# A two-layer graph attention network on one core: two more aggregates split on two levels, and the second-level left sums made in halves from a pool of their own

## The chip, the cores and the metric

The kernel runs on one core of one Trainium2 chip. The metric is the device time of one execution in microseconds. One execution was also taken by the hardware profiler; its page and its trace are what this document reads. The engines are TensorE (PE; its weight loads are PEld), VectorE (DVE), ScalarE (ACT), GpSimd (POOL) and SyncE (SP). Each engine takes its own list of instructions in order. In this kernel SP issues the loads, and POOL issues nearly all the stores and some of the loads.

## The reference

```python
h = jnp.maximum(_layernorm(x), 0.0)            # x: 2708 x 1024, float32
f = h @ Wf + bf;  g = h @ Wg + bg
scores = where(adj > 0, relu(f @ g.T), NEG)
x = x + softmax(scores, axis=1) @ (h @ W + bW)
h = jnp.maximum(_layernorm(x), 0.0)
h2 = h @ W1
scores = where(adj > 0, leaky_relu(h2 @ a1 + (h2 @ a2).T, 0.2), NEG)
out = x + relu(softmax(scores, axis=1) @ h2)
```

Everything is float32; adj is a 2708 x 2708 matrix of zeros and ones.

## The kernel before, in words

**Panels and products.** The kernel works with transposed attention matrices: the 2708 destination rows are the columns of five panels p = 0 to 4, with 576, 576, 532, 512 and 512 columns, and the source rows stand on the partitions, as ten pairs of 128-row tiles (q = 0 to 9) and a small rest (`left_over`). The large matrix products use a scheme with seven half-size products, M1 to M7, in place of eight, whose operands are sums and differences of the quarters. Two matmul records in the trace stand for one float32 matmul.

**Layer 0.** For each panel: `scores(p)` (products sx, sy, sz, ten steps q), then `project_q(p+1)` for the next panel's right side, then `aggregate(0, p)` (attention times h, products gx, gy, gz, gv), then `project(0, p)` (times W, plus residual and bias, result x1). project(0,3) stands after scores(4). In `scores`, VectorE's work is held in program order (`nc.hold`).

**Aggregates.** `aggregate` uses one level of seven products: each has ten pairs q by four blocks d, with a right side of half the panel's width h. Its left rows come by SP from DRAM (`hc`), where `rows_h` and `sums_h` put the seven sums of each pair (`hg_d`, one array for two pairs). `aggregate_quartered` splits each of the seven products into seven again: five blocks k by two blocks d, with a right side of h/2. `quarters_of` makes its right sides, and its left sides are rows (`hr_d`) or sums of four quarters of rows (`hs2_d`). Before the change it serves panels 1 to 4 of layer 1 only.

**Second-level left sums.** `put_quarters(m, k)` is one such task: POOL loads four quarter rows (`hq<-hr_d`), VectorE makes four additions of 128x256 (`add` and `sub`), POOL stores the result (`hs2_d`, in the profile `hs_d<-hq`). There are 7 x 5 = 35 tasks, with two loads and two stores of 256 KB each. They lie in the list `lazy`, from which `behind` takes work behind a stage's matmuls while `spare[0]` is set. The rows of layer 1 are written by `pair_h` (sums g1, g2: `g` in the profile, and `hr_d<-g`) as soon as `finish0` has a pair of finished x1 rows. One block k needs the rows of two neighbouring pairs.

**Order.** A list scheduler reorders what isn't held in program order, within what buffers and data allow. Buffers of a pool go round in the order of the program. The pools are `slots` (54 buffers, work tiles), `strm` (12, what is streamed in: hc, As, w, hq and others) and a few small ones.

**Residual.** `finish0` loads x (SP), and POOL adds the bias to it in SBUF by an accumulating DMA; the projected rows are then added and stored to x1.

Of the kernel before, what the change touches and what calls it, by code (L numbers as in the profile page):

```python
# [57 lines left out]
def kernel(  # L58
# [60 lines left out]
    strm = ctx.enter_context(tc.tile_pool(name="strm", bufs=12))  # L119
# [8 lines left out]
    def stream(name, shape=(P, D), dt=FP):  # L128
        return strm.tile(list(shape), dt, tag="strm", name=name)

# [23 lines left out]
    groups = [[q, q + 1] for q in range(0, NQ, 2)]  # L154
    group_of = {q: (i, j) for i, g in enumerate(groups) for j, q in enumerate(g)}
    assert sorted(group_of) == list(range(NQ))
    hg_d = [dram.tile([P, 7, len(g), W], FP, name=f"hg_d{i}") for i, g in enumerate(groups)]
    NK = NQ // 2
    WH = W // 2
    hr_d = dram.tile([P, 7, 2, 2, NK, WH], FP, name="hr_d")  # L160
    hs2_d = dram.tile([P, 7, 4, NK, WH], FP, name="hs2_d")

    def rows_at(m, q):

        return hr_d[:, m, :, q % 2, q // 2]
# [30 lines left out]
    spare, from_slots = [False], [False]  # L196
# [4 lines left out]
    def one(of=None):  # L201
        of = later if of is None else of
        for it in of[:4 if of is lazy and from_slots[0] else ahead[0]]:
            if it[1]:
                it[1]()
                it[1] = None
        us, _, go = of.pop(0)[:3]
        go()
        return us
# [114 lines left out]
    def pair_h(q, ha, hb):  # L324

        n = P
        on = nc.vector
        if q >= NQ - F // 2:
            s1, s2, s3, s4 = (slot(f"g{i}")[:, :W] for i in range(4))
            for m, h in ((M1, ha[0]), (M2, hb[0]), (M4, hb[1])):  # L330
                store(rows_at(m, q), as_blocks(h))
            on.tensor_tensor(s1, ha[1], hb[1], OP.add)
            on.tensor_tensor(s2, s1, ha[0], OP.subtract)
            for m, h in ((M5, s1), (M6, s2)):
                store(rows_at(m, q), as_blocks(h))

            def rest():
                on.tensor_tensor(s4, hb[0], s2, OP.subtract)
                on.tensor_tensor(s3, ha[0], ha[1], OP.subtract)
                for m, h in ((M3, s4), (M7, s3)):  # L340
                    store(rows_at(m, q), as_blocks(h))
            return rest
        g1, g2 = stream("g1", (P, 2, W)), stream("g2", (P, 2, W))
        s1, s2, s3, s4 = g1[:n, 0], g1[:n, 1], g2[:n, 0], g2[:n, 1]
        on.tensor_tensor(s1, ha[1], hb[1], OP.add)
        on.tensor_tensor(s2, s1, ha[0], OP.subtract)
        on.tensor_tensor(s3, ha[0], ha[1], OP.subtract)
        on.tensor_tensor(s4, hb[0], s2, OP.subtract)
        for m, h in ((M1, ha[0]), (M2, hb[0]), (M4, hb[1])):
            store(rows_at(m, q), as_blocks(h))  # L350
        store(rows_at(slice(M5, M6 + 1), q), as_blocks(g1[:n]))
        store(rows_at(slice(M7, M3 + 1), q), as_blocks(g2[:n]))

    def rows_h(q, ha, hb):

        i, j = group_of[q]
        for m, h in ((M1, ha[0]), (M5, ha[1]), (M2, hb[0]), (M4, hb[1])):
            store(hg_d[i][:, m, j], h)
# [3 lines left out]
    def sums_h():  # L362

        def fetch(q, two):
            i, j = group_of[q]
            for m in (M1, M2):
                two.append(stream("hr", (P, 2, W)))
                load(two[-1], hg_d[i][:, m:m + 2, j])

        def first(q, two):  # L370
            (a0, a1), (b0, b1) = ((t[:, 0], t[:, 1]) for t in two)
            add(b1, a1, b1)
            sub(a1, a0, a1)

        def second(q, two):
            (a0, a1), (b0, b1) = ((t[:, 0], t[:, 1]) for t in two)
            sub(a0, b1, a0)
            sub(b0, b0, a0)
            i, j = group_of[q]
            store(hg_d[i][:, M6:M7 + 1, j], two[0])  # L380
            store(hg_d[i][:, M3, j], b0)
            store(hg_d[i][:, M5, j], b1)
            summed[0] += 1
        for q in range(NQ):
            two = []
            put(1.4, lambda q=q, two=two: first(q, two), lambda q=q, two=two: fetch(q, two))
            put(1.4, lambda q=q, two=two: second(q, two))

    BY_QUARTERS = (M1, M5, M2, M6, M7, M3, M4)
    made_quarters = {}  # L390

    def put_quarters(m, k, to=lazy):

        two = []

        def fetch():
            if from_slots[0]:
                two.extend(slot(f"hq{h}", (P, 2, WH)) for h in range(2))
            else:
                t = stream("hq", (P, 4, WH))  # L400
                two.extend(t[:, 2 * h:2 * h + 2] for h in range(2))
            for h in range(2):
                nc.gpsimd.dma_start(two[h], hr_d[:, m, h, :, k])

        def go():
            a11, a12, a21, a22 = (two[h][:, i] for h in range(2) for i in range(2))
            add(a22, a21, a22)
            sub(a21, a11, a21)
            sub(a11, a22, a11)
            sub(a12, a12, a11)  # L410
            for h in range(2):
                store(hs2_d[:, m, 2 * h:2 * h + 2, k], two[h])
            made_quarters[m] = made_quarters.get(m, 0) + 1
        put(1.7, go, fetch, to=to)

    def quarters_until(m):
        while made_quarters.get(m, 0) < NK:
            one(lazy if lazy else later)
# [465 lines left out]

    def aggregate(l, p, S, sm, then={}, rate=3.0):
# [28 lines left out]
        def left(m, q, d):  # L914
            i, j = group_of[q]
            if (m, i) not in hc:
                hc[m, i] = stream("hc", (P, 4, WH) if l else (P, 2, W))
                load(hc[m, i], hr_d[:, m, :, :, i].rearrange("p h f c -> p (h f) c") if l else hg_d[i][:, m])
            return hc[m, i][:, d // 2 * 2 + j, d % 2 * P:(d % 2 + 1) * P] if l else hc[m, i][:, j, d * P:(d + 1) * P]
# [67 lines left out]
    def quarters_of(p, S):  # L987
# [9 lines left out]
        def operand(m, q):  # L997
            if m in (M5, M4):
                return t1(q)
            s = wa_(q) if m in (M1, M6, M7) else wb_(q)  # L1000
            return s[:, hi if m in (M3, M7) else lo]
# [27 lines left out]
        def second():  # L1029
            for q in range(NQ):  # L1030
                sub(wa_(q)[:, lo], wb_(q)[:, hi], t1(q))
            for q in range(NQ):
                sub(wa_(q)[:, hi], wb_(q)[:, hi], wa_(q)[:, hi])

        def fourth():
            for q in range(NQ):
                sub(t1(q), wb_(q)[:, lo], wa_(q)[:, lo])
        return {"make": make, "right": right, "first": first, "fifth": fifth, "second": second, "fourth": fourth}

    def aggregate_quartered(p, S, sm, of_right, then={}, fine=1.2):  # L1040
# [12 lines left out]
        def product(m, n, ps, start):  # L1053
            quarters_until(m)
            if (m, 0) not in lasts:
                for i, of in enumerate((hr_d[:, m, :, :, NK - 1].rearrange("p h f c -> p (h f) c"), hs2_d[:, m, :, NK - 1])):
# [5 lines left out]
            load(t, hr_d[:, m, i // 2, i % 2, :NK - 1] if raw else hs2_d[:, m, i, :NK - 1])  # L1062
# [11 lines left out]
        def left_over(banks, e, s, fresh):  # L1074

            two = stream("hl", (P, W + 2 * P))
            load(two, hgl_d[1][:, e])
# [44 lines left out]
        def with_second():  # L1122
# [3 lines left out]
        before_next = {M1: lambda: make(M5), M5: with_second, M2: lambda: (of_right["fourth"](), make(M6)), M6: lambda: make(M7),  # L1126
                       M7: lambda: make(M3), M3: lambda: make(M4)}
        left_out = None
        for m in BY_QUARTERS:
            V = [quad(*direct[m])[:, 2 * r:2 * r + 2] for r in range(2)] if m in direct else [v[:, :, :h] for v in in_pairs("V")]  # L1130
# [40 lines left out]
            if m == M5:  # L1171
                of_right["second"]()
            if m == M5:
                inverse.append(inverse_sums(p, sm))
# [178 lines left out]
    def scores(p, B):  # L1353
# [49 lines left out]
        for q in range(NQ):  # L1403
# [3 lines left out]
            if q + 2 <= LEFT:  # L1407
                fetch(q + 2)
            sa, sb = slot("Sa"), slot("Sb")
# [111 lines left out]
    def rows_done(t, xt):  # L1521
# [14 lines left out]
        if panel_of[t] == NP - 1:  # L1536
# [9 lines left out]
            else:  # L1546
# [12 lines left out]
                if q == NQ - 1:  # L1559
                    for m in BY_QUARTERS:  # L1560
                        put_quarters(m, q // 2, later)
# [17 lines left out]
        elif whole:  # L1579
# [3 lines left out]
            if quads_met[q // 2] == 2:  # L1583
                put(0.0, lambda: [put_quarters(m, q // 2) for m in BY_QUARTERS])
# [8 lines left out]

    def finish0(p):
        xs, seen = {}, {}

        def start(ts):
            for t in ts:
                if p == NP - 1:
                    first_mask[t] = load_mask(0, *pair_of[t])  # L1600
                if t == TINY:
# [7 lines left out]
                xs[t] = row_halves("x_res", t == MONO)  # L1609
                load_rows_of(t, xs[t], x)  # L1610
# [27 lines left out]

    got = {}
# [29 lines left out]
    for p in range(NP):  # L1669
        got["S"], got["acc"] = scores(p, B)  # L1670
# [20 lines left out]
        spare[0], from_slots[0] = p > 0, p == NP - 1  # L1691
        G[p] = aggregate(0, p, S, got["sm"], then)
        spare[0] = False
        if p == 0:
            flush()
            ahead[0] = 2
# [98 lines left out]
    for p in range(NP):  # L1795
# [6 lines left out]
        g = aggregate_quartered(p, S, sm, next_right, then, fine=1.0) if p else aggregate(1, p, S, sm, then, rate=4.0)  # L1802
# [34 lines left out]
```

## Time and profile before

| | |
|---|---|
| median of 3 runs | 3094.57 us (3094.34 to 3098.68) |
| the profiled execution | 3099.78 us, its span 3098.0 us |
| TensorE busy | 3002.8 us, 97% of the span |
| VectorE, ScalarE, POOL busy | 2070.7, 463.2, 506.3 us |
| DMA | 764.70 MB, mean 247 GB/s; SP's queue 62.0% and POOL's 16.4% of 16 engines' span |
| mean granted TensorE clock | 0.989 |

The span runs from the first to the last instruction; the execution's own time has 1.8 us around it. Busy times are shares of one execution, and the stages differ: the stretches of the span have to be read one by one, cut where the stages change. The layer-0 aggregates of panels 2 and 3 lie at 1262 to 1399 us and 1639 to 1771 us. Releasers in the profile are inferred from semaphore events, and a pair of names such as `hq<-hr_d` is output and input of an instruction.

### The profile page before, as it was taken

Reading aid. Unit: us, or ns where it says so; the run is one execution under the profiler, and the core shown is the slowest. Engines: PE = TensorE matmul, PEld = TensorE weight load, DVE = VectorE, ACT = ScalarE, POOL = GpSimd, SP = SyncE. Lnnn points to the kernel's source line nnn. Section 1 sums busy time; section 2 is a strip of 40 time slices with the busy share of each in tenths; the row PEclk is TensorE's granted clock in tenths of the full one; section 3 lists DMA queues with packets and bytes.
Section 4 is the critical chain, followed back from the end, with each engine's and each line's share of the span. In section 5 each row is a group of like instructions: output and inputs, shape, how many; then the busy total and the mean of one; then the engine's idle time right before and its main releaser. Section 6 shows DMA issues by size and latency. Waiting matters only on the chain.

```text
span 3098.0 us, 41680 instructions
## 1 busy us (share of the span) xinstructions
PE 3002.8 (97%) x14630; PEld 2298.1 (74%) x14630; DVE 2070.7 (67%) x4615; ACT 463.2 (15%) x817; POOL 506.3 (16%) x786
## 2 busy tenths in 40 slices
PE   8998999899999999999999999997999999999998
PEld 4576777657877588885888886783777969879694
DVE  5767693776651596716975277766968768887853
ACT  3420020010110101101011001301222121212200
POOL 1421101310011110214101001141202010020202
PEclk9999999999999999999999999998999999999999
DMA  6999967998565796758967577789667868888896
GB/s 225 291 257 254 301 247 253 309 274 229 178 238 153 217 260 223 244 158 241 278 199 255 164 217 234 237 266 350 229 216 249 274 202 296 287 269 294 264 297 246
DMA packets 448577, 764.70 MB, mean 247 GB/s; under 512 B 175776, under 2 KB 262592, under 8 KB 448368
## 3 DMA queue, kind: packets, MB, share of 16 engines
q1 hardware_dynamic: 393008, 598.31, 62.0%
q0 software_dynamic: 55360, 163.73, 16.4%
q8 instruction: 116, 1.90, 0.3%
q14 instruction: 93, 0.76, 0.1%
HBM read 627.95 MB, written 133.91 MB: 246 GB/s over the span
## 4 chain that ended last, share of the span: by engine, by line
PE 71%; DVE 11%; DMA 7%; issue 7%; SPq 2%; POOL 1%; ACT 1%; POOLq 0%; DVEq 0%; ACTq 0%
PE sz L1378 6%; PE gx L661 6%; PE gy L661 6%; PE gz L661 5%; PE gz L1067 5%; PE pz L1267 4%; PE sx L1378 4%; PE sy L1378 4%; PE px L1267 4%; PE py L1267 3%; PE gx L1067 3%; PE gy L1067 3%; PE M_ps L574 3%; PE qz L661 2%; PE qx L661 2%
## 5 line engine op out<-in xcount | busy, mean ns | idle before, releaser
L1378 PE MATMUL sz<-B,As 128*128 128x288 f32 (+2 forms) x1200 | 293.5, 394 | 11.8 <-DVE st L45 8.8
L1378 PEld LDWEIGHTS sz<-B,As 128*128 128x128 f32 x1200 | 227.8, 191 | 61.8 <-DVE st L45 12.7
L1378 PE MATMUL sx<-B,As 128*128 128x288 f32 (+2 forms) x800 | 199.6, 392 | 6.4 <-DMA As<-hs_d 4.4
L1378 PE MATMUL sy<-B,As 128*128 128x288 f32 (+2 forms) x800 | 199.3, 392 | 2.3 <-DMA As<-hs_d 2.3
L661 PE MATMUL gz<-Sa,hc 128*128 128x288 f32 (+2 forms) x800 | 189.2, 397 | 6.3 <-DMA hc<-hg_d 6.3
L661 PEld LDWEIGHTS gz<-Sa,hc 128*128 128x128 f32 x800 | 153.8, 193 | 40.1 <-DMA hc<-hg_d 6.8
L1378 PEld LDWEIGHTS sx<-B,As 128*128 128x128 f32 x800 | 151.3, 190 | 40.1 <-DMA As<-hs_d 3.7
L1378 PEld LDWEIGHTS sy<-B,As 128*128 128x128 f32 x800 | 152.0, 190 | 33.4 <-issue 2.7
L1067 PE MATMUL gz<-quarter,hc 128*128 128x128 f32 (+2 forms) x1344 | 168.8, 279 | 3.8 <-DVE gT L45 3.7
L143 POOL DMA_DIRECT2D out_dram<-x_res x180 | 89.0, 501 | 482.1 <-DVE x_res L45 474.7
L1067 PEld LDWEIGHTS gz<-quarter,hc 128*128 128x128 f32 x1344 | 160.6, 191 | 5.1 <-DVE gT L45 4.6
L1267 PE MATMUL px<-w,gT 128*128 128x512 f32 x320 | 143.9, 602 | 7.5 <-DMA w<-in_L_gnn_W_dram 6.0
L1267 PE MATMUL pz<-w,ps 128*128 128x512 f32 x320 | 142.1, 594 | 0.8 <-DVE pt L45 0.8
L1267 PE MATMUL py<-w,ps 128*128 128x512 f32 x320 | 142.0, 593 | 0.0
L143 POOL DMA_DIRECT2D mk_d<-mask x55 | 35.8, 652 | 534.8 <-DVE mask L45 528.1
L1267 PEld LDWEIGHTS px<-w,gT 128*128 128x128 f32 x320 | 60.9, 193 | 80.9 <-issue 74.7
L1267 PEld LDWEIGHTS pz<-w,ps 128*128 128x128 f32 x320 | 60.2, 190 | 77.1 <-issue 70.7
L1267 PEld LDWEIGHTS py<-w,ps 128*128 128x128 f32 x320 | 60.5, 190 | 75.8 <-issue 73.9
L574 PE MATMUL M_ps<-wgT,wfT 128*128 128x512 f32 x256 | 113.5, 600 | 1.6 <-ACT hsT L45 1.6
L661 PE MATMUL gy<-T,hc 128*128 128x288 f32 (+2 forms) x480 | 111.6, 394 | 0.0
L977 POOL TENSOR_TENSOR gT<-gT,rr 128x2304 f32<-128x2304 f32 (+5 forms) x12 | 44.4, 3700 | 382.4 <-DVE rr L45 179.8
L661 PEld LDWEIGHTS gy<-T,hc 128*128 128x128 f32 x480 | 91.2, 190 | 19.5
(377 smaller groups left out, 5803.6 us busy)
## 6 DMA issues: line engine op xcount, KB each, us to landing
hc<-hg_d SPq DMA_DIRECT2D x175, 512.0 KB
As<-hs_d SPq DMA_DIRECT2D x150, 512.0 KB
hc<-hr_d SPq DMA_DIRECT2D x119, 512.0 KB
hc<-hs_d SPq DMA_DIRECT2D x112, 512.0 KB
w<-wt_d SPq DMA_DIRECT2D x96, 512.0 KB
w<-in_L_gnn_W_dram SPq DMA_DIRECT2D x72, 512.0 KB
md<-md_d SPq DMA_DIRECT2D x56, 512.0 KB
adj_i<-in_adj_dram SPq DMA_DIRECT2D x200, 128.0 KB
```

The lines of the kernel that those rows point to most:

```text
L143: nc.gpsimd.dma_start(a, b)
L574: nc.tensor.matmul(ps, wfT[a][c // NH][:, c % NH, :], wgT[b][c], start=(c == 0), stop=(c == NC - 1))
L661: nc.tensor.matmul(ps[d], left(m, k, d), right(m, k), start=(start and k == 0), stop=(k == K - 1), skip_group_check=True)
L977: nc.gpsimd.tensor_tensor(of(e, s), of(e, s), by(s, k), OP.mult)
L1067: nc.tensor.matmul(ps[:, d], lhs[:, d * P:(d + 1) * P], inner_right(m, n, k), start=(start and k == 0 and d == 0), stop=(k == NK - 1), ski ...
L1267: nc.tensor.matmul(ps, left[i][m][:, k, :], w_[k], start=(start and k == 0), stop=(k == NH - 1), skip_group_check=True)
L1378: nc.tensor.matmul(ps[:n, :h], lefts[q][:, i % 2, c, :n], B[m][c // 2][:, c % 2, :h], start=(start and c == 0), stop=(c == NH - 1), skip_g ...
```

## The change

- The layer-0 aggregates of panels 2 and 3 are made by `aggregate_quartered`. M1 and M5 stay one-level products (through `accumulate`), and M2, M6, M7, M3 and M4 are split again. `quarters_of` loses the separate buffer for M4's right side.
- The rows of layer 0 move from `hg_d` to `hr_d[0]`, in the layout of layer 1 (pieces of 1 KB in place of 2 KB), and layer 0 gets second-level sums of its own, `hs2_d[0]`. Their tasks are queued after aggregate(0,0) in the program's text; `spare[0]` is set again after aggregate(0,1).
- `put_quarters` makes each task in two halves of 128 columns: one load and one store by POOL of 256 KB, four additions of 128x128, in a buffer from a new pool `side` with four buffers. Layer 1 has 70 such half-tasks, layer 0 has 50. At most three are fetched ahead.
- `strm` has 10 buffers in place of 12. `from_slots` goes.
- For panels 2 and 4 (`ORDERED`) the residual is prepared in DRAM during `scores`: POOL copies x to x1_d and adds the bias there by accumulating DMAs, in program order, and `finish0` loads the sum by SP.

The diff, cut to its core (the moves from `hg_d` to `hr_d[0]` in `rows_h`, `sums_h` and `aggregate` only change the address):

```diff
-    strm = ctx.enter_context(tc.tile_pool(name="strm", bufs=12))
+    strm = ctx.enter_context(tc.tile_pool(name="strm", bufs=10))
+    side = ctx.enter_context(tc.tile_pool(name="side", bufs=4))
...
-    hr_d = dram.tile([P, 7, 2, 2, NK, WH], FP, name="hr_d")
-    hs2_d = dram.tile([P, 7, 4, NK, WH], FP, name="hs2_d")
+    hr_d = [dram.tile([P, 7, 2, 2, NK, WH], FP, name=f"hr{l}_d") for l in range(2)]
+    hs2_d = [dram.tile([P, 7, 4, NK, WH], FP, name=f"hs2{l}_d") for l in range(2)]
...
-        for it in of[:4 if of is lazy and from_slots[0] else ahead[0]]:
+        for it in of[:3 if of is lazy else ahead[0]]:
...
-    BY_QUARTERS = (M1, M5, M2, M6, M7, M3, M4)
+    BY_QUARTERS = [(M2, M6, M7, M3, M4), (M1, M5, M2, M6, M7, M3, M4)]
...
+    def put_quarters(l, m, k, to=lazy):
+        for half in range(2):
+            two = []
+            cs = slice(half * P, (half + 1) * P)
+
+            def fetch(two=two, cs=cs):
+                two.append(aside("hq", (P, 4, P)))
+                nc.gpsimd.dma_start(two[0].rearrange("p (h f) c -> p h f c", h=2), hr_d[l][:, m, :, :, k, cs])
+
+            def go(two=two, cs=cs):
+                a11, a12, a21, a22 = (two[0][:, i] for i in range(4))
+                add(a22, a21, a22)
+                sub(a21, a11, a21)
+                sub(a11, a22, a11)
+                sub(a12, a12, a11)
+                store(hs2_d[l][:, m, :, k, cs], two[0])
+                made_quarters[l, m] = made_quarters.get((l, m), 0) + 1
+            put(0.9, go, fetch, to=to)
...
         def second():
             for q in range(NQ):
-                sub(wa_(q)[:, lo], wb_(q)[:, hi], t1(q))
+                sub(wa_(q)[:, hi], wb_(q)[:, hi], wa_(q)[:, hi])
             for q in range(NQ):
-                sub(wa_(q)[:, hi], wb_(q)[:, hi], wa_(q)[:, hi])
+                add(wa_(q)[:, lo], wa_(q)[:, hi], wa_(q)[:, lo])
...
+        if l == 0:
...
+            exps_until(NQ)
+            of_right["fifth"]()
+            accumulate(left, of_right["operand"], NQ, h, (M1, M5), then,
+                       {M1: first_product, M5: lambda d, ps: add(quad(0, hi)[:, d], ps, quad(0, lo)[:, d])}, "g",
+                       {M5: sums_of_columns}, rate=rate, by_k=True, more={(M5, NQ // 2): with_second})
+
         left_out = None
-        for m in BY_QUARTERS:
+        for m in BY_QUARTERS[l]:
...
+            if p in ORDERED:
+                ts = tiles_of(p)
+                copy_residual(p, ts[q:q + 1])
+                bias_residual(p, ts[q - 4:q - 3] if q > 3 else [])
...
+    ORDERED = (2, NP - 1)
+
+    def by_gpsimd(o, i, **k):
+        tc.keep_in_program_order(nc.gpsimd.dma_start(o, i, **k))
...
+                if p in ORDERED:
+                    for e in range(2):
+                        load(xs[t][e], x1_d[t][:, e * W:(e + 1) * W])
+                    continue
...
+    SPLIT_EARLY = (2, 3)
...
     for p in range(NP):
+        spare[0] = False
         got["S"], got["acc"] = scores(p, B)
...
-        spare[0], from_slots[0] = p > 0, p == NP - 1
-        G[p] = aggregate(0, p, S, got["sm"], then)
-        spare[0] = False
+        spare[0] = p > 0
+        if p in SPLIT_EARLY:
+            G[p] = aggregate_quartered(0, p, S, got["sm"], quarters_of(p, S), then)
+        else:
+            G[p] = aggregate(0, p, S, got["sm"], then)
+        spare[0] = p == 1
         if p == 0:
             flush()
+            for m in BY_QUARTERS[0]:
+                for k in range(NK):
+                    put_quarters(0, m, k)
```

## The prediction

> **What bounds the kernel now.** I read the engine totals first.
>
> ```profile
> PE 3002.8 (97%) x14630; PEld 2298.1 (74%) x14630; DVE 2070.7 (67%) x4615; ACT 463.2 (15%) x817; POOL 506.3 (16%) x786
> ```
>
> TensorE is busy 97% of the span: what removes TensorE rows pays in full, and what makes TensorE wait costs in full. Next the table of stretches, cut at the stages (columns: from and to, length; busy PE, PEld, DVE, ACT, POOL; clock; DMA share; GB/s).
>
> ```profile
> 600.00:812.00 212.00, 207.87 (x800) 143.18 (x799) 143.03 (x308) 12.20 (x21) 27.49 (x39) 1.00 0.88 244
> 864.00:1012.00 148.00, 148.00 (x629) 114.10 (x628) 47.90 (x110) 6.05 (x13) 27.81 (x28) 1.00 0.67 199
> ...
> 1262.00:1399.00 137.00, 137.00 (x629) 114.13 (x628) 45.40 (x109) 5.00 (x11) 29.02 (x32) 1.00 0.69 208
> ...
> 1639.00:1771.00 132.00, 132.00 (x630) 114.16 (x629) 45.39 (x111) 4.24 (x10) 18.92 (x19) 1.00 0.71 217
> ...
> 2083.00:2160.00 77.00, 58.08 (x141) 26.95 (x140) 48.67 (x122) 10.01 (x17) 20.81 (x30) 0.88 1.03 349
> ...
> 2562.00:2690.00 128.00, 125.33 (x1125) 123.11 (x1124) 103.26 (x287) 23.07 (x43) 4.38 (x10) 1.00 0.87 296
> ```
>
> In order: project(0,0) with scores(1); aggregates p=1, 2 and 3 of layer 0, one level of seven products; project(0,4), the one stage here that TensorE doesn't fill; aggregate p=2 of layer 1, two levels. Aggregates have a free VectorE (45 of 137 us) and a full TensorE; scores stages have both nearly full. Inside aggregate p=2 of layer 0, and of layer 1, the chain of waits has one product each:
>
> ```profile
> 1280.33 17.93 PE gy L661 x80
> ```
>
> ```profile
> 2616.55 4.53 PE gz L1067 x40
> ```
>
> A record costs 17.93/80 = 224.1 ns at 266 columns and 4.53/40 = 113.3 ns at 133. (p=3: 17.27/80 = 215.9 and 4.47/40 = 111.8.) Last, the second-level left sums "hq": their groups, the answer for their tile, and a timeline of VectorE in aggregate p=1.
>
> ```profile
> L143 POOL DMA_DIRECT2D hs_d<-hq x70 | 50.3, 721 | 60.1 <-DVE hq L45 56.8 <-DMA hs_d<-hq 1.7 <-DMA hq<-hr_d 1.0
> L403 POOL DMA_DIRECT2D hq<-hr_d x70 | 50.1, 718 | 200.9 <-PE qy L661 115.6 <-PE qz L661 45.7 <-DVE P L45 29.7
> ```
>
> ```profile
> DMA to landing us min/median/max: 2.6/4.9/11.5
> ```
>
> ```profile
> 875.01 8.46 DVE L45 TENSOR_TENSOR hq<-hq 128x256 f32<-128x256 f32 x25
> ```
>
> Today the loads wait for nobody but their ring's turn, and 25 sums run in a row, with PE at 148.00 of 148: the round trips are covered.
>
> **What the Trainium skill says.** "Perfetto Trace Analysis", Sequencer Loop: a sequencer takes instructions one after another and each waits for its semaphores; so an add that waits for a load holds all behind it on VectorE. "DMA: Bandwidth & Descriptors", Two DMAs through the same engine are not ordered: the issuing engine must wait on the first DMA's semaphore before it issues a dependent one; so POOL stands still between a store of rows and the load of them. Same page, Anatomy of one DMA: 2.0 us plus bytes over 436 GB/s, 2.6 us for 256 KB; the trace's fastest hq landing is 2.6, its median 4.9. "VectorE: DVE Perf Modes", The TRN2 errata: a fixed cost per instruction, so halved tiles cost more; the trace agrees: 8.46/25 = 338 ns at 256 columns, and 207 ns at 128 columns (rows of that shape in a run), where half of 338 would be 169.
>
> **The change, part by part.** All against the profiled execution, 3099.8 us (span 3098.0); it stands 5.2 above the median of the runs, 3094.57.
>
> *Five of seven products split again, p=2 and 3.* A product has 10 pairs x 4 x 2 records = 80 today, and 7 x 5 x 2 x 2 = 140 after. p=2: 400 x 224.1 ns = 89.6 us becomes 700 x 113.3 = 79.3, −10.3. p=3: 400 x 215.9 = 86.4 becomes 700 x 111.8 = 78.3, −8.1. Layer 1's two-level stages wait for VectorE's evictions 2.4 us each, which I charge: −18.4 + 4.9 = **−13**. VectorE's added evictions (103 us busy in layer 1's stage against 45 here) fit beside 130 us of TensorE. Left reads rise by 10 MB a stage, 28.5 to 38.5 MB, to some 300 GB/s: layer 1 runs at 296 with TensorE full. Streaming buffers 12 to 10: the prefetch gets a sixth shorter, charged nothing, since no hc wait shows in these stages; were that cover gone, a wait of the size of the one hc wait in the trace (6.3 us) per stage.
>
> *Residual of p=2 and 4 prepared in DRAM during scores.* It takes x loads (SP) and accumulating bias DMAs (POOL) out of project. For p=2 TensorE hides them today: 0. Project(0,4) idles 19 us at DMA share 1.03; **−4** (0 to −12). The 20 or so DMAs added to POOL in scores(2) and scores(4) at 0.5 to 0.75 us are 15 us of a queue 10 to 15% busy: 0, but see below what it costs to stand behind a waiting POOL.
>
> *Left sums.* There are 50 new half-tasks for layer 0 (rows of five products, five blocks each) and 70 half-tasks in place of 35 for layer 1. VectorE work: 200 x 0.207 = 41 us new, and 280 x 0.207 − 140 x 0.338 = 11 us more. That alone would hide in the aggregates. What counts is place. Before, hq shares the streaming pool, whose buffers go round in program order and so hold the tasks where the program puts them. After, its pool of four serves nothing else, and in the built program's order the tasks have moved to as early as their rows exist. Ten stand in the start and scores(0), four by project_q(1), 32 in aggregate(0,0) (20 ahead of VectorE's m<-gv, some 31 ahead of m<-gy). Of layer 1's, twelve of each block of 14 stand in a burst right behind the last g of their rows: in scores(1), (2) and (3), then aggregate(0,4) and layer 1's aggregate p=0. On POOL they alternate load, store, each load waiting for the store two tasks earlier.
>
> Prices: the load and store landings are not seen in that arrangement. From below 2.6 us each; from above the medians, 4.9 loading and 6.9 storing. I take 3.5 and 4.5, since a stalled TensorE stops SP's reads and the queues empty. POOL issue: 0.72 us today, the new shape has twice the pieces; 1.0, between 0.72 and 1.4.
>
> Scores(1), the timeline of VectorE where the burst will stand, after the last g:
>
> ```profile
> 690.54 0.68 DVE L45 TENSOR_TENSOR g<-x_res,g 128x512 f32<-128x512 f32 x1
> 691.14 0.45 DVE L45 TENSOR_TENSOR Sb<-sz,st 128x288 f32<-128x288 f32 x1
> ...
> 694.18 1.66 DVE L45 SCALAR_TENSOR_TENSOR mx<-maskl,f,mx 128x576 f32<-128x576 bf16 x2
> 695.76 0.82 DVE L45 TENSOR_TENSOR sm<-sx,rb 128x288 f32<-128x288 f32 x2
> ```
>
> Today 4.6 us pass from g's end to sm<-sx. After, g must be stored (its landing takes 6.4) and loaded (1.0 + 3.5): 10.9 us to the first sum. A task then costs half of store issue, landing and load issue, (1.0 + 4.5 + 1.0)/2 = 3.25. In scores(1) 36 adds, nine tasks, stand ahead of sm<-sx: 10.9 + 29.2 − 4.6 = 35.5 late. TensorE can go on for the three products that need no late bank, 1.8 to 1.9 us each, 5.5: **+30**. Scores(3) has 23 adds, six tasks: 10.9 + 19.5 − 3.4 − 5.5 = 21.5, and 6 for the six tasks behind: **+28**. In scores(2) twelve tasks spread over 1.35 steps of 13.6 us: 39 − 18 − 5.5 = 15.5, and some for g's round trip: **+18**. Sum 76 (ends, by both bounds: 32 and 110).
>
> Aggregate(0,0): a rotation of four costs 1.0 + 3.5 + 0.8 + 1.0 + 4.5 = 10.8 us, 2.7 a task; 31 tasks from 472, where the first-level sums end, put m<-gy at 556 in place of 526.5. Some 44 us of VectorE work lie between it and gT<-gy (58 less 14 idle), plus four tasks, 11: gT at 611 in place of 584.4, and TensorE waits for gT there already (sum_ps, 4.3 us). **+22**, a little under 26 (5 to 45).
>
> Start and scores(0): hq loads stand on POOL behind just-issued row stores and ahead of three hs_d<-hsT stores, which feed As; each holds POOL 6.4 + 1, partly lead: **+15** (5 to 30). Aggregate(0,4): **+2** (0 to 5). Layer 1's aggregate p=0 gets its last twelve where VectorE is busy 126 of 157: **+10** (0 to 17).
>
> Sum: −13 − 4 + 76 + 22 + 15 + 2 + 10 = +108; 3208 on this execution, **3203** on the median. All losses at the low ends give 42 − 17 = +25, 3120; at the high ends 207 − 17 = +190, 3285.
>
> **Rivals.** (a) *Faster.* The early sums use idle VectorE, as the 25 in a row at 875 do with TensorE full; only the gains remain: 3094.6 − 17 = 3078. It decides if VectorE is never held longer than TensorE's lead of 5.5 us in scores and DMA landings overlap. For it: idle VectorE in aggregates. Against: in scores VectorE shows no idle between g and sm, and a round trip through DRAM of at least 2.6 + 2.6 + issues is already longer than the lead. (b) *Slower, mildly:* the round trips run at the fastest landings, 3120. (c) *DMA becomes the bound:* scores(0) already has a DMA share of 0.98 at 289 GB/s, and 14 tasks of 0.5 MB add 7 MB, 24 us more: 3227; against it, the share after a stall falls. (d) *The placement isn't what counts,* and buffers 12 to 10 make the split aggregates wait for left rows: 6.3 us on each of the ten split products would be +63 − 17, 3141; no hc wait in layer 1's two-level stages speaks for it.
>
> **Numbers.** 0.2% (6 us) is about what a measurement here can tell from no change. The main case 0.55, (b) 0.20, (c) 0.08, (d) 0.05, (a) 0.09 and 0.03 for losses that just eat the gains. So faster 0.09, same 0.03, slower 0.88. The range takes (b), the main case's ends, (c) and (d): 3106 (the low end with the residual's −12 and no wait in the split stages) to 3285.
>
> **What would show it.** Right: VectorE's idle before hq, 11.4 us today, above 100 by hq<-hr_d; TensorE waiting for sm, Sb or st in scores(1) to (3) and for m or gT in aggregate(0,0); the stretch of scores(1) some 30 us longer; split stages near 129 and 126 us with TensorE full. Wrong: those VectorE waits short, or split stages no shorter than 137 and 132, or a wait for hc in them.

## The result and the profile after

The changed kernel takes 3291.17 us (median of four runs, 3287.09 to 3291.72) against 3096.62: a ratio of 1.0627, 95% interval 1.0614 to 1.0640, 195 us slower. The forecast was slower by 108. Its profiled execution has a span of 3289.9 us, 191.9 above the one before.

The engine totals of the changed kernel, and its costliest new group (busy, mean of one; then VectorE's idle time ahead of it and what ended that):

```profile
PE 3028.7 (92%) x15358; PEld 2335.6 (71%) x15358; DVE 2199.4 (67%) x5213; ACT 469.5 (14%) x837; POOL 576.4 (18%) x876
...
L45 DVE TENSOR_TENSOR hq<-hq 128x128 f32<-128x128 f32 x480 | 123.3, 289 | 219.0 <-DMA hq<-hr_d 213.9
```

Two things are to be seen. VectorE's wait for left sums rose from 11.4 us to 213.9. And TensorE's busy time rose by 26 us although the split took rows away: the same work ran slower.

The table of stretches of the changed kernel (columns as in the prediction), cut at the first product of each stage (aggregate(0,0); project(0,0); scores(1); scores(2); aggregate(0,2); scores(3); aggregate(0,3); project(0,4)):

```profile
467.80:682.60 214.80, 163.21 (x646) 122.27 (x645) 129.62 (x359) 6.92 (x14) 88.44 (x120) 0.86 0.88 302
682.60:740.60 58.00, 50.46 (x114) 22.00 (x113) 32.60 (x67) 7.22 (x12) 10.97 (x15) 0.94 0.87 236
740.60:935.40 194.80, 155.96 (x629) 118.63 (x628) 120.23 (x285) 4.17 (x8) 34.00 (x50) 0.89 0.75 220
1196.90:1379.40 182.50, 147.72 (x630) 119.65 (x629) 120.76 (x297) 4.01 (x7) 41.79 (x57) 0.91 0.88 257
1429.00:1555.90 126.90, 126.90 (x995) 120.25 (x993) 71.90 (x209) 8.26 (x21) 0.45 (x2) 1.00 0.74 235
1609.90:1782.10 172.20, 139.12 (x629) 117.00 (x628) 127.38 (x292) 4.89 (x9) 38.11 (x54) 0.91 0.85 256
1831.40:1963.00 131.60, 127.42 (x993) 121.68 (x992) 70.77 (x211) 7.58 (x20) 1.31 (x2) 0.97 0.76 232
2285.50:2351.00 65.50, 53.77 (x134) 24.55 (x132) 48.02 (x118) 10.77 (x19) 17.58 (x26) 0.89 0.93 327
```

Of the two split stages only aggregate(0,2) is full of TensorE (126.9 of 126.9, 10 us shorter than before). The scores stages stand idle longer and run at a lower clock (the third column from the end, the share of the full clock that TensorE was granted: 0.89, 0.91, 0.91). Scores(1), (2) and (3) before, for comparison:

```profile
660.50:812.40 151.90, 148.06 (x630) 113.68 (x629) 105.05 (x228) 4.13 (x8) 13.03 (x21) 1.00 0.82 236
1074.00:1212.50 138.50, 136.39 (x629) 113.71 (x628) 108.29 (x246) 4.01 (x7) 14.17 (x20) 1.00 0.88 254
1452.20:1590.00 137.80, 132.30 (x630) 113.60 (x629) 114.50 (x236) 4.84 (x9) 18.25 (x28) 1.00 0.91 271
```

Cut the same way in all profiles, the stages moved so against the profile before (us; a stage runs from its first product to the first product of the next; a dash is under 2):

| stage | before | changed | layer 1's sums alone on the side pool, no split | layer 0's alone there | all in the streaming pool | whole tasks, streaming pool, residual of panel 4 alone |
|---|---|---|---|---|---|---|
| start to project_q(1) | 445.9 | +22 | -8 | +26 | -3 | -3 |
| aggregate(0,0) + project(0,0) | 214.6 | +58 | +10 | +56 | - | - |
| scores(1) | 151.9 | +43 | +44 | -2 | -2 | -2 |
| aggregate(0,1) | 148.1 | - | - | - | +58 | +50 |
| scores(2) | 138.6 | +44 | +39 | +23 | +23 | - |
| aggregate(0,2) | 137.0 | -10 | - | +4 | - | -10 |
| project(0,2) | 52.9 | - | - | - | - | +15 |
| scores(3) | 137.8 | +34 | +34 | -2 | - | - |
| aggregate(0,3) | 132.0 | - | - | +10 | +8 | -8 |
| aggregate(0,4) | 133.6 | +8 | +8 | +10 | +7 | - |
| project(0,4) | 75.8 | -10 | -10 | -5 | - | -10 |
| layer 1's aggregate p=0 | 152.9 | - | - | +18 | +16 | - |

The first row moves by some 7 us from profile to profile whatever the kernel, and isn't read finer. Scores(1) moves by some 2 us in the same way. From aggregate(0,1) on, most stages that nothing touches agree to 0.1 us, which is what makes this table useful.

**Scores(1), the main mechanism.** The changed kernel's timeline of VectorE, from the last g on:

```profile
775.12 0.69 DVE L45 TENSOR_TENSOR g<-x_res,g 128x512 f32<-128x512 f32 x1
786.16 0.94 DVE L45 TENSOR_TENSOR hq<-hq 128x128 f32<-128x128 f32 x3 [10.36 <-DMA hq<-hr_d]
...
788.94 0.45 DVE L45 TENSOR_TENSOR Sb<-sz,st 128x288 f32<-128x288 f32 x1
...
799.37 1.27 DVE L45 TENSOR_TENSOR hq<-hq 128x128 f32<-128x128 f32 x4 [3.31 <-DMA hq<-hr_d]
...
817.69 0.81 DVE L45 TENSOR_TENSOR sm<-sx,rb 128x288 f32<-128x288 f32 x2
```

The first sum waits 10.4 us for g's way through DRAM (10.9 was forecast), and sm<-sx comes 41.9 us after g's end (41.9 - 4.6 = 37.3 late, 35.5 forecast). That the lateness is so near the forecast is in part luck: 48 additions, twelve tasks, stand ahead of sm<-sx, not the 36 of nine, and they take 31.5 us, 2.6 a task and not 3.25. The same stretch on TensorE:

```profile
789.44 6.28 PE L1399 MATMUL sz<-B,As 128*128 128x288 f32 x16 [13.79 <-DVE Sb L45]
795.56 2.10 PE L1399 MATMUL sy<-B,As 128*128 128x288 f32 x8
818.56 4.21 PE L1399 MATMUL sx<-B,As 128*128 128x288 f32 x8 [20.89 <-DVE sm L45]
822.56 3.08 PE L1399 MATMUL sz<-B,As 128*128 128x288 f32 x8
825.47 2.10 PE L1399 MATMUL sy<-B,As 128*128 128x288 f32 x8
```

TensorE waits 13.8 and 20.9 us. After the first wait 16 records take 6.28 us, after the second eight take 4.21 and the next eight 3.08; eight take 2.10 a little later. The stretches after the second wait show why (columns as above):

```profile
820.00:823.00 3.00, 3.00 (x7) 1.93 (x7) 3.00 (x6) 0.00 (x0) 0.00 (x0) 0.50 0.01 4
823.00:826.00 3.00, 3.00 (x11) 2.21 (x10) 2.55 (x8) 0.00 (x0) 0.00 (x0) 0.75 0.33 63
826.00:830.00 4.00, 4.00 (x18) 3.16 (x17) 3.19 (x8) 0.00 (x0) 0.55 (x1) 1.00 0.82 281
```

After this wait the granted clock is half, for about 6 us from the restart at 818.6. The Trainium skill says so ("TensorE: Matmul & The Clock Gate", Part 1: The HAM clock gate): the array's clock falls to half after an idle window of about 3.4 us and returns after about as long of steady work. The trace agrees in kind, with 0.50, 0.75 and then 1.00; the return took longer here than the page's figure. The prediction had left this out.

### The profile page after: what moved, and what is told of

It is laid out like the page before. It is cut to its first block, busy times and chain, and to the rows that moved or that the text cites. A ratio compares the mean times of both kernels' runs of the same rounds, so it can differ in the third digit from the quotient of the medians.

```text
span 3289.9 us, 43809 instructions
## 1 busy us (share of the span) xinstructions
PE 3028.7 (92%) x15358; PEld 2335.6 (71%) x15358; DVE 2199.4 (67%) x5213; ACT 469.5 (14%) x837; POOL 576.4 (18%) x876
## 3 DMA queue, kind: packets, MB, share of 16 engines
q1 hardware_dynamic: 458800, 619.28, 60.6%
## 4 chain that ended last, share of the span: by engine, by line
PE 60%; DVE 12%; DMA 10%; issue 8%; POOL 3%; ACT 1%; SPq 1%; POOLq 0%; DVEq 0%; ACTq 0%
PE gz L1063 7%; PE sz L1399 6%; PE gx L1063 4%; PE gy L1063 4%; PE sx L1399 4%; PE sy L1399 4%; PE gx L653 4%; PE gy L653 3%; PE qz L653 3%; PE gz L653 3%; DMA hq<-hr_d 3%; PE px L1288 3%; PE pz L1288 3%; PE py L1288 3%; DVE P L45 2%
## 5 line engine op out<-in xcount | busy, mean ns | idle before, releaser
L1399 PE MATMUL sz<-B,As 128*128 128x288 f32 (+2 forms) x1200 | 303.2, 403 | 42.8 <-DVE Sb L45 29.1
L1399 PE MATMUL sx<-B,As 128*128 128x288 f32 (+2 forms) x800 | 214.2, 413 | 70.7 <-DVE sm L45 49.0
L45 DVE TENSOR_TENSOR hq<-hq 128x128 f32<-128x128 f32 x480 | 123.3, 289 | 219.0 <-DMA hq<-hr_d 213.9
L1399 PEld LDWEIGHTS sx<-B,As 128*128 128x128 f32 x800 | 159.3, 201 | 109.9 <-DVE sm L45 51.5
L1063 PE MATMUL gz<-quarter,hc 128*128 128x128 f32 (+2 forms) x1824 | 228.5, 279 | 3.8 <-DVE gT L45 3.7
L1063 PEld LDWEIGHTS gz<-quarter,hc 128*128 128x128 f32 x1824 | 217.5, 191 | 5.3 <-DVE gT L45 4.5
L653 PE MATMUL gz<-Sa,hc 128*128 128x288 f32 (+1 forms) x480 | 125.0, 423 | 43.4 <-DMA hc<-hr_d 35.6
L653 PEld LDWEIGHTS gz<-Sa,hc 128*128 128x128 f32 x480 | 97.3, 204 | 70.7 <-DMA hc<-hr_d 36.6
L147 POOL DMA_DIRECT2D hs_d<-hq x120 | 92.6, 773 | 175.5 <-DVE hq L45 163.3
L396 POOL DMA_DIRECT2D hq<-hr_d x120 | 91.1, 762 | 118.4 <-DMA hs_d<-hq 67.7
```

The source lines that it names most:

```text
L45: i = f(*a, **k)
L147: nc.gpsimd.dma_start(a, b)
L396: nc.gpsimd.dma_start(two[0].rearrange("p (h f) c -> p h f c", h=2), hr_d[l][:, m, :, :, k, cs])
L653: nc.tensor.matmul(ps[d], left(m, k, d), right(m, k), start=(start and k == 0), stop=(k == K - 1), skip_group_check=True)
L1063: nc.tensor.matmul(ps[:, d], lhs[:, d * P:(d + 1) * P], inner_right(m, n, k), start=(start and k == 0 and d == 0), stop=(k == NK - 1), ski ...
L1399: nc.tensor.matmul(ps[:n, :h], lefts[q][:, i % 2, c, :n], B[m][c // 2][:, c % 2, :h], start=(start and c == 0), stop=(c == NH - 1), skip_g ...
```

## The experiments

**1. The tasks back in the streaming pool.**

```diff
-    strm = ctx.enter_context(tc.tile_pool(name="strm", bufs=10))
-    side = ctx.enter_context(tc.tile_pool(name="side", bufs=4))
+    strm = ctx.enter_context(tc.tile_pool(name="strm", bufs=12))
...
-        return side.tile(list(shape), dt, tag="side", name=name)
+        return strm.tile(list(shape), dt, tag="strm", name=name)
```

> The changed kernel with one difference: the half-tasks of the left sums take their buffer from the streaming pool (12 buffers again) and there is no side pool. The scheduler then leaves them where the program puts them: all 50 of layer 0 in aggregate(0,1), layer 1's in the aggregates of layer 0 and in layer 1's aggregates p=0. The same 120 tasks, the same additions, the same DMAs. Theory A (the place of the tasks is what costs): the start, scores(0) to (3) and aggregate(0,0) are back at their times before, the gains stay (aggregate(0,2) -10, project(0,4) -10): 3096.6 - 20 = 3076, between 3066 and 3086; VectorE waits for hq<-hr_d under 30 us, PE's clock again 0.985 or more. Theory B (the tasks' work costs, 480 additions, 240 DMAs on POOL and 61 MB of traffic there, wherever it stands): over 3200.

3208.41 us, ratio 1.0359 (1.0337 to 1.0381): a miss, and in the range of theory B. By stage theory A was right in part. The tasks are back in the aggregates, and scores(1), scores(3) and aggregate(0,0) are back at their times before, so their place did cost those stages their time. But aggregate(0,1), which now holds 64 half-tasks, is 58 us longer, and TensorE waits 36.7 us there for left rows hc. Waits of SP in it:

```profile
SPq L142 <- DMA hs_d<-hq: 118.9, 24, 20.6
```

SP's next load needs a streaming buffer that a sum keeps until its store has landed, and the left rows stand behind it. A new wait took the place of the old one. Scores(2) stays 23 us longer too, without a sum in it; experiment 5 takes that up.

**2. Side pool kept, tasks held in program order.**

```diff
-                nc.gpsimd.dma_start(two[0].rearrange("p (h f) c -> p h f c", h=2), hr_d[l][:, m, :, :, k, cs])
+                by_gpsimd(two[0].rearrange("p (h f) c -> p h f c", h=2), hr_d[l][:, m, :, :, k, cs])
...
+                held, nc.hold = nc.hold, ("vector",)
                 add(a22, a21, a22)
...
+                nc.hold = held
-                store(hs2_d[l][:, m, :, k, cs], two[0])
+                by_gpsimd(hs2_d[l][:, m, :, k, cs], two[0])
```

> The changed kernel with the side pool of four and 10 streaming buffers as they are, but every addition, load and store of a half-task is held in program order. Theory A (place): as when the tasks are in the streaming pool, 3076 to 3090, since the tasks come in the aggregates, where round trips on a ring of four (about 2.7 us a task, 64 tasks in 148 us of aggregate(0,1)) are hidden. Theory B (the ring of four buffers, or the 10 streaming buffers, make the waits wherever the tasks stand): over 3150, with VectorE waiting over 100 us for hq<-hr_d.

3245.65 us, ratio 1.0484 (1.0467 to 1.0501): missed, and as theory B had it, with 178.8 us of waits for hq on VectorE in the whole kernel. Aggregate(0,1) is 66 us longer, now with no wait for left rows at all; TensorE waits 57.6 us for gT, whose evictions stand on VectorE among sums that wait 89.2 us in 58 waits. POOL waits 78.6 us in 56 waits for stores to land before it may load: the ring's rate, 64 tasks in 148 us, wasn't reached.

**3. and 4. Layer 1's tasks alone early, and layer 0's alone.**

```diff
-    SPLIT_EARLY = (2, 3)
+    SPLIT_EARLY = ()
...
-            for m in BY_QUARTERS[0]:
-                for k in range(NK):
-                    put_quarters(0, m, k)
```

```diff
-                two.append(aside("hq", (P, 4, P)))
+                two.append((stream if l else aside)("hq", (P, 4, P)))
```

> The changed kernel without the split of the aggregates p=2 and 3 of layer 0 and without the 50 tasks of layer 0; the 70 half-tasks of layer 1 on the side pool stay, and so does the residual. Theory A with costs that add up by stage, from the changed kernel's stretches: scores(1) +43, scores(2) +44, scores(3) +34, aggregate(0,4) +8, project(0,4) -10, all else 0: +119, 3216 (3200 to 3230). Rival (the tasks of layer 0, crowding POOL and the ring, are what makes those of layer 1 late): under 3140.

> The changed kernel with layer 1's half-tasks in the streaming pool (10 buffers), and layer 0's in the side pool, so that only layer 0's are early. Theory A with costs that add up by stage: project_q(0) +13, scores(0) +14, project_q(1) -4, aggregate(0,0) +49, project(0,0) +9, aggregate(0,2) -10, project(0,4) -10, start -1: +60, 3157 (3142 to 3172). Rival (as above, one list of tasks makes the other late): the cost is shared otherwise, over 3200 or under 3130.

3222.71 us (ratio 1.0417, 1.0399 to 1.0434) and 3244.00 us (1.0481, 1.0465 to 1.0497). The first is near its forecast, and by stage scores(1), scores(3) and aggregate(0,4) are those of the changed kernel: layer 1's bursts cost what they cost whatever layer 0 does. The second missed by 87 us and lies in the range of its rival. Its first stages came as forecast (+26 and +56), but stages that hold layer 1's half-tasks, now in the streaming pool, or that stream beside them are longer (layer 1's aggregate p=0 +18, the split stages +4 and +10), and scores(2) stays 23 longer with no sum in it.

**5. and 6. The residual alone,** as a part of the kernel before.

```diff
+            if p in ORDERED:
+                ts = tiles_of(p)
+                copy_residual(p, ts[q:q + 1])
+                bias_residual(p, ts[q - 4:q - 3] if q > 3 else [])
...
+    ORDERED = (2, NP - 1)
```

Experiment 6 has `ORDERED = (NP - 1,)`.

> The kernel before with one part of the change: the residual of panels 2 and 4 prepared in DRAM during scores(2) and scores(4). Theory: the 23 us by which scores(2) is longer even where no left sum stands in it (it was +22 to +23 in the kernels with the sums in the streaming pool, the pinned ones, and the one with layer 0's alone early) is the residual's DMAs, which delay the rows As; and project(0,4) gives 10 back: 3096 + 23 - 10 = 3109 (3103 to 3116). Rival (the residual is free in scores, the 23 us come from the new layout of the rows or the shorter streaming pool): 3086 (3082 to 3090).

> The kernel before with the residual prepared in DRAM for panel 4 alone. Scores(4) was unchanged in every kernel with it, project(0,4) 10 us shorter where nothing else stood in it: 3086 (3083 to 3090), faster than before. Rival (the gain is given back in the next stage): 3096.

3109.09 us against 3095.95 (ratio 1.0039, 1.0027 to 1.0052) and **3086.13 us** (0.9965, 0.9951 to 0.9979). Both came as expected. In the first scores(2) is 17 us longer and project(0,4) 9.7 shorter. TensorE's largest wait there, which the kernel before doesn't have:

```profile
PE sx L1378 <- DMA As<-hs_d: 10.8, 4, 4.6
```

The copies and accumulating DMAs went into a stage with a DMA share of 0.88 and made the rows As late. Scores(4), at 0.75, took the same without loss. That the DMA share decides is inferred from these two stages; no run varies it alone. The second kernel, with panel 4 alone, is the one version here that beats both, by some 10 us.

**7. One held VectorE.** The kernel before, with a wait put into scores(1):

```diff
...
+            if p == 1 and q == 5:
+                nc.vector.memset(held, 0.0)
+                for _ in range(3):
+                    nc.gpsimd.dma_start(held_d, held)
+                    nc.gpsimd.dma_start(held, held_d)
+                nc.vector.tensor_copy(held2, held)
```

> The kernel before, and in scores(1), at step q = 5, VectorE is made to wait once, in its program order, for three round trips of a 2 KB tile through DRAM on POOL (six DMAs, some 12 to 20 us). Theory: the kernel loses the wait H, less TensorE's lead of about 5.5 us, plus a toll of 3 to 5 us because TensorE's granted clock is at half after it has stood still: H - 1, say 3111 for H = 16. Rival (no toll): H - 5.5, and TensorE busy the same 3003 us.

3111.44 us, 15.5 more (ratio 1.0048, 1.0034 to 1.0061). The wait of VectorE, TensorE's wait (longest 14.9), the stretch of scores(1), and TensorE's total:

```profile
DVE held L45 <- DMA held<-held_d: 19.6, 1, 19.6
```

```profile
PE sx L1381 <- DVE sm L45: 15.3, 2, 14.9
```

```profile
654.80:823.90 169.10, 150.30 (x629) 114.90 (x628) 104.97 (x230) 4.12 (x8) 16.25 (x27) 0.96 0.69 212
```

```profile
PE 3005.5 (97%) x14630; PEld 2299.8 (74%) x14630; DVE 2070.5 (67%) x4617; ACT 463.1 (15%) x817; POOL 508.6 (16%) x792
```

TensorE's lead was 19.6 - 14.9 = 4.7 us (5.5 in the forecast). With H = 19.6 the total is nearer the rival (H - 5.5 = 14.1 us more) than the theory (H - 1 = 18.6). But TensorE's busy time, which the rival had unchanged, rises: by 2.2 us in this stage (150.30 against 148.06, at a clock of 0.96 against 1.00) and by 3005.5 - 3002.8 = 2.7 in all. So there is a toll of slower clock, and it is smaller than the 3 to 5 us expected. The stage is 17.2 us longer, 14.9 of waiting and 2.2 of toll.

**8. Whole tasks as before the change,** in 12 streaming buffers, residual for panel 4 alone: the edit puts back the old `put_quarters`, with the layer as an argument, and sets `ORDERED = (NP - 1,)`.

> The changed kernel with the left sums as before the change: whole tasks of 128x256 with two loads and two stores, in the streaming pool of 12, the 25 tasks of layer 0 in aggregate(0,1) beside seven of layer 1; residual prepared for panel 4 alone. Theory (a task in the streaming pool costs what its buffer is kept from the left rows, and half-tasks keep a whole buffer each for half the work): aggregate(0,1) loses half of the 58 us that it lost with half-tasks, or less, +15 to +30; layer 1's aggregate p=0 is back at its time; aggregate(0,2) -10, (0,3) -3 to -8, project(0,4) -10: 3093 (3080 to 3105). Rival (the loss is in the additions and bytes, the same in both forms): +58, 3130.

3139.26 us, ratio 1.0136 (1.0120 to 1.0153): the rival was nearer. Aggregate(0,1) loses 50 us with 32 whole tasks where it lost 58 with 64 halves; SP waits 118.4 us there for hs_d<-hq. The split stages give 10.2 and 7.9 us, what the sum had for TensorE (10.3 and 8.1). Project(0,2) loses 14.7, which the prediction had no term for; TensorE waits 11.8 of them for W's rows. SP's list there:

```profile
1422.88 28.28 SPq L139 DMA_DIRECT2D x_res<-in_x_dram  x48
...
1455.44 2.07 SPq L139 DMA_DIRECT2D w<-wt_d  x4
```

Behind a split aggregate, whose own loads keep SP busy, the 48 small loads of x come late and W's rows stand behind them. That is what the residual of panel 2 takes away (project(0,2) is +1 in the changed kernel); it costs 17 in scores(2) and saves about 14 here.

**9. and 10. More buffers:** eight in the side pool and eight streaming (seven tasks fetched ahead); four and 12, with 50 work buffers in place of 54.

> The changed kernel with eight buffers in the side pool, seven fetched ahead, and eight streaming buffers. The tasks stand as early as before. Theory (a burst costs the round trip of the rows plus a rate set by the ring, half of store issue, landing and load issue per task): the rate part shrinks; scores(1) +25 in place of +43, scores(2) +30 for +44, scores(3) +20 for +34, aggregate(0,0) +35 for +49: 3240 (3220 to 3260). Rival (the place alone costs, since VectorE waits for the first round trips whatever the ring): 3280 to 3300.

> The changed kernel with 12 streaming buffers beside the side pool of four, and 50 work buffers in place of 54 to make room. Theory: the wait for left rows in the split aggregate(0,3) goes (-8 in place of 0), and aggregate(0,0) loses less, since a streaming buffer held by w_rows is a smaller part of the pool: 3270 (3258 to 3283); the bursts in scores stay. Rival (buffers don't matter): 3291. If the 12 buffers took most of the loss away (under 3200), the shorter streaming pool would be the cause and not the place of the tasks.

3381.26 us (ratio 1.0922, 1.0896 to 1.0947) and 3279.74 us (1.0590, 1.0569 to 1.0612): the first missed, above both its theory and its rival, the second is as expected. With eight on the side scores(1) is +30 in place of +43, as the rate of the ring would have it. But scores(2) is +52 and scores(3) +37, not less, scores(0) is +30, aggregate(0,3) +20, and TensorE waits 60.6 us for As: eight streaming buffers look too few. The two changes aren't separated, so the rate of the ring isn't shown. With 12 streaming buffers 11 us come back, 6 of them in aggregate(0,3); the bursts stay (+39, +40, +35). The shorter streaming pool is a small part of the loss, as far as the four work buffers given up cost nothing.

**11. The ring of eight, held in order, layer 0 only;** layer 1's tasks as before the change, residual for panel 4, 10 streaming and 50 work buffers.

> The split with layer 1's sums as before the change (whole tasks in the streaming pool), layer 0's 50 half-tasks held in program order in a side pool of eight (50 work and 10 streaming buffers), residual prepared for panel 4 alone. Theory (64 half-tasks at some 2.7 us are 173 us and don't fit behind aggregate(0,1)'s 148; 50 on a ring of eight, at half of that, are some 70 us and fit): aggregate(0,1) +5 to +20, (0,2) -10, project(0,2) +15, (0,3) -8, project(0,4) -10: 3096 (3085 to 3107). Rival (the 25 tasks cost 50 us in an aggregate wherever their buffers are): 3130 to 3140.

3189.44 us, ratio 1.0298 (1.0274 to 1.0322): missed, and above its rival too, with aggregate(0,1) +66 and project(0,2) +18. TensorE waits 23.4 us for gT, 20.8 for left rows hc and 14.0 for hl. Under every pool tried, the work of 25 more whole tasks cost aggregate(0,1) 50 to 66 us.

**12. w_rows loaded by POOL,** a test of aggregate(0,0).

```diff
-        load(t, w[c * P:(c + 1) * P, :])
+        (nc.gpsimd.dma_start if name == "w_rows" else load)(t, w[c * P:(c + 1) * P, :])
```

> The changed kernel with the loads of w_rows in aggregate(0,0) issued by POOL and not by SP. Theory: SP stood 29 us at such a load, whose streaming buffer was held by weight sums behind the left sums on VectorE, and the left rows hc stood behind it: that wait (28 us) goes, and aggregate(0,0) with project(0,0) loses 30 in place of 58: 3263 (3250 to 3275). Rival (the evictions behind the left sums on VectorE set the end, and hc would only wait elsewhere): 3285 to 3295.

3282.22 us, ratio 1.0593 (1.0570 to 1.0616): missed, near the rival. Aggregate(0,0) is +43 for +49, and hc is still waited for (31.4 us), with SP standing 77.8 us in this stretch at stores of weight sums (`wt_d<-w_rows`). The weight sums come as late as in the changed kernel (from 590 us on), and changing who issues the load doesn't give back the buffer sooner.

**13. to 15. The additions on POOL:** of all tasks; of layer 0's alone; of all, with 12 streaming and 50 work buffers.

```diff
-                add(a22, a21, a22)
+                by = nc.gpsimd
+                by.tensor_tensor(a22, a21, a22, OP.add)
...
```

Experiment 14 has `by = nc.vector if l else nc.gpsimd`.

> The changed kernel with the additions of all left sums made by POOL (GpSimd) in place of VectorE; loads, stores, pools and the number of tasks are the same. VectorE then never waits for hq. Theory (the bulk of the loss is VectorE held, and TensorE's clock after it): scores(1) and (3) lose under 10 in place of 43 and 34, scores(2) keeps 17 to 22 for the residual, aggregate(0,0) under 20 in place of 49: 3160 (3110 to 3190), TensorE's clock 0.98 or more. Rival (POOL's queue and the DMA traffic make late what the others wait for, VectorE only shows it): over 3240.

> The same for layer 0's tasks alone; layer 1's stay on VectorE. Theory for aggregate(0,0): its evictions stand behind the left sums on VectorE, so +49 becomes under +20 and the total 3260 (3245 to 3272). Rival (POOL stands at the loads and keeps back the stores of first-level rows and of weight sums, which left rows and SP wait for): aggregate(0,0) keeps +40 or more, 3280 to 3310.

> All left sums on POOL, with 12 streaming and 50 work buffers. Theory: as with all on POOL, less what the 12 buffers gave the changed kernel (11 us, most of it in aggregate(0,3)): 10 below the kernel with all sums on POOL. Rival: no difference.

3257.66 us (ratio 1.0521, 1.0494 to 1.0548), 3305.61 (1.0684, 1.0663 to 1.0704) and 3242.31 (1.0477, 1.0454 to 1.0500). The first two missed and lie in the ranges of their rivals, which put the loss on POOL's queue and the DMAs. With VectorE free of sums, scores(1), (2) and (3) are +24, +28 and +16 in place of +43, +44 and +34. So VectorE standing at the sums is about half of it, or more, since POOL got work besides. The rest isn't taken apart: in scores(1) VectorE waits 13.5 us for one instruction of POOL's, and in scores(2) TensorE waits 22.5 for As. Aggregate(0,0) goes the other way, +73 (+76 in experiment 14). TensorE's waits in the first of these kernels, and SP's list there:

```profile
PE gz L654 <- DMA hc<-hr_d: 72.1, 2, 69.2
```

```profile
552.50 68.69 SPq L143 DMA_DIRECT2D w_rows<-in_L_gnn_W_dram  x2
621.28 0.99 SPq L143 DMA_DIRECT2D hc<-hr_d  x1
```

The changed kernel shows the same two waits, smaller (TensorE; SP):

```profile
PE gz L653 <- DMA hc<-hr_d: 35.6, 2, 28.0
```

```profile
SPq L143 <- DMA wt_d<-w_rows: 50.7, 8, 29.4
```

In both kernels SP stands at a load into a streaming buffer that isn't free until a store of weight sums (`wt_d<-w_rows`) has landed, and the left rows hc stand behind SP. But what makes that store late isn't the same. VectorE's first weight sum in the kernel before and in the changed one, then POOL's and SP's lists in the changed one:

```profile
528.82 0.68 DVE L45 TENSOR_TENSOR wT<-w_rows 128x512 f32<-128x512 f32 x1
```

```profile
594.76 0.68 DVE L45 TENSOR_TENSOR wT<-w_rows 128x512 f32<-128x512 f32 x1
```

```profile
597.18 0.56 POOL L147 DMA_DIRECT2D wt_d<-wT  x1
597.73 0.56 POOL L147 DMA_DIRECT2D wt_d<-w_rows  x1
```

```profile
573.50 0.33 SPq L143 DMA_DIRECT2D w_rows<-in_L_gnn_W_dram  x1
603.28 0.38 SPq L143 DMA_DIRECT2D hc<-hr_d  x1
```

In the changed kernel the weight sums stand on VectorE behind left sums, which wait 55.8 us there for their loads. They come 44 us later in the stage than before, and POOL issues the store of each 2 to 4 us after it starts. So VectorE sets this wait. In experiment 13 VectorE starts its first weight sum at 551.9 us, but POOL, busy with the additions, issues the first of these stores at 617.2. Giving POOL the sums handed the wait from one queue to the other; it doesn't show that POOL's queue set it before, though the total lies in that rival's range. The last kernel is 15 us below the first of these, near the 10 that the longer pool was to give.

## Why the prediction was wrong

The sign, the main mechanism and most of its places were right; the sum was 108 where 195 were measured (192 between the profiles), above the range's end of 3285. By its terms:

| term | forecast | measured |
|---|---|---|
| start, scores(0), project_q(1) | +15 | +22 |
| aggregate(0,0), project(0,0) | +22 | +58 |
| bursts in scores(1), (2), (3) | +76 | +121, of it some 17 the residual in scores(2) |
| aggregate(0,4); layer 1's aggregate p=0 | +12 | +8 |
| split of two aggregates | -13 | -10 |
| residual, project(0,4) | -4 | -10 |

- **The bursts' waits were sized well; what follows a wait was not.** TensorE's idle time rose by 35, 33 and 28 us in scores(1) to (3) (length less busy time in the two tables of stretches), 95 in all and about 80 without the 16 us of waits for As in scores(2), against 76. That they fit so well is luck in part: more additions stood ahead of sm<-sx than forecast (48 for 36 in scores(1), 33 for 23 in scores(3)), at a lower price each. The other 26 us are busy time, 8 + 11 + 7: the clock. The step that failed is the one that turns a wait of VectorE into time ("TensorE can go on for the three products ..., 5.5"): it took the lead off and added no toll for the restart. Over the whole kernel the toll is the rise of busy time plus what the split took away, 25.9 + 18.1 = 44 us, half of the shortfall. Counted in the traces, TensorE is busy at half clock for 119 us where it was for 40, and half of that difference is 40. Experiment 7 has one such stop alone, at 2.2 to 2.7 us.
- **Costed at nothing: the residual's DMAs in scores(2).** The step looked at POOL's issue time (15 us in a queue 10 to 15% busy) and not at the DMA share of 0.88. It measured +17 (experiment 5). What it saves in project(0,2), some 14, was costed at nothing too, since TensorE covered it before; behind a split aggregate that cover is gone (experiment 8).
- **Aggregate(0,0): VectorE later than forecast, and another wait at its end.** The forecast followed VectorE's lateness to m and gT. The 31 tasks ahead of m<-gy were counted right, but they began 7 us later in the stage and took 2.9 us each, not 2.7: m<-gy is 45 us late, 30 were forecast. TensorE waits only 7.7 and 3.4 us for m and gT; its largest wait is hc, 35.6 us, by way of the weight sums that stand behind the left sums on VectorE, a streaming buffer and SP. The prediction didn't name the weight sums. The lists of experiment 13 and of the changed kernel show this path; how much POOL's queue adds stays open. So does what the start and scores(0) lost beyond the forecast, which no run takes apart.
- **The split was right** where it could be seen: 10.2 in the changed kernel and 10.2 and 7.9 in experiment 8, against 10.3 and 8.1. Its 4.9 us of eviction waits didn't come. In the changed kernel panel 3's gain was lost to waits for hc (4.1 us) and the clock after them; 12 streaming buffers bring 6 back. That is rival (d)'s mechanism, at a tenth of its price.
- **Layer 1's aggregate p=0** was charged 10 and lost nothing; VectorE was busy 124 of 152 us there.
- **Rival (a), the sums finding room in the aggregates,** would have failed too, and more widely than argued: put there, they cost 50 to 66 us (experiments 1, 2, 8, 11). That the 28 additions of seven tasks ran unseen there before didn't mean that the 128 of 32 would.

## What to carry to other kernels

Before moving work to a pool of its own, ask what the old pool's turn-taking held in place: here it was what kept loads, sums and stores out of the stages with no slack. Follow a stall through every queue that shares a buffer with it, and add for each stop of TensorE what it loses at half clock afterwards. A small edit that only moves DMAs is to be judged in the stage that it moves them into, where the DMA share is the first thing to look at.

## What the runs showed of the hardware that was not expected

One stop of 14.9 us cost 2.2 us of TensorE's time in its stage beyond the stop (experiment 7), and a kernel with many stops ran at a mean granted clock of 0.962 against 0.989. A 128x128 addition took 0.29 us on VectorE (mean of 480) and 0.46 us on POOL (median, experiment 13); the changed kernel with all of them on POOL was 34 us faster all the same. Where both engines added at once there (554 to 562 us), POOL's 128x128 took 0.9 us, and VectorE's 128x512 took 0.94 where it takes 0.69 in the changed kernel. POOL's DMA issue with twice the pieces took 0.75 us (median of 120, 0.72 before), not the 1.0 assumed.
